# Attention sums accumulated key tile by key tile, or all at the end of a batch

## The chip, the cores and the metric

The kernel runs on one core of a Trainium2 chip. A core has five engines that take their instructions in order, each from a queue of its own, and that wait for each other through semaphores: TensorE (PE in the profile; its weight loads are PEld), VectorE (DVE), ScalarE (ACT), GpSimd (POOL) and SyncE (SP), which here issues nearly all transfers. The metric is device time in microseconds (us), the median of several runs; less is better.

## The reference

The input is x of shape (32, 512, 128) and a symmetric 0/1 adjacency of shape (32, 512, 512). Four layers follow each other, each as x = x + layer(relu(layernorm(x)), adjacency). The change lies in the first, an attention whose mask is the adjacency:

```
v = relu(x Wv + bv);  q = relu(x Wq + bq);  k = relu(x Wk + bk)
h = clip((q k^T) * mask, 0, CLAMP_HI) - NEG_PENALTY * (1 - mask)
out = softmax(h, axis=2) @ v
```

The second layer is a graph convolution with an LSTM over 128 rows, taken from the last 128 nodes of each batch; the third is four graph layers with tanh; the fourth is a product with the adjacency and a PReLU. For the change it matters that the attention of one query is a sum over the 512 keys of exp(score) times mask times v, divided by the sum of exp(score) times mask.

## The kernel before, in words

The path that runs is `symmetric` (line 772); `general` (line 39) is a fallback for other inputs. The work of the 32 batches is cut in four:

- `pass_1(b)` (line 1126) computes keys and values of a batch and the attention of its last 128 queries alone, which the LSTM needs, and stores keys, values and normed input in DRAM (f_dkq, f_dv).
- `lstm()` (line 1220) makes 128 steps for all batches together. A step is a chain from engine to engine: a product on PE (f_z, line 1234), tanh on ACT (1260, 1272), two cell operations on DVE (1266, 1267), tanh on ACT (1274), and the output with its transpose on DVE (1278, 1279), after which the next step's product can start.
- `pass_2(b)` (line 1289) does the attention of the other 384 queries, in three tiles of 128. It loads the stored data and the mask, makes the queries (f_pq, 1316, and f_q, 1319 or 1320), and for each of the four key tiles j a scores product (f_s, 1325), its exponential on ACT (f_e, 1328), and the mask on DVE (1329). Then come twelve products with the values (f_po, 1334): for each query tile t, four that add up over j. The values carry a column of ones, so that the sum of the exponentials comes out in column 128. DVE takes its reciprocal (1338) and updates x (1340), which is stored as f_dx (1345). For batches 0 to 21 (`EARLY`), the sums over the graph (f_pg, 1419) are made in pass 2 too.
- `rest(b, turn, ...)` (line 1433) does all that needs the LSTM's result. The first two turns take batches 26 and 27 (`FIRST`). Its steps that matter here are f_plw and f_pl (1470, 1477), f_gT (1481), a norm, the turned rows f_xt_c (872), and per graph layer f_py (1523, its bank filled with a bias by line 967 or 971), f_y (1402, 1403), f_pa (1419, 1530, 1534). It also stores the adjacency (f_das, 1491), reads it back transposed (f_aT, 1493), and compares both on DVE (f_junk, 1496).

Each f_s, f_pq, f_po and f_z product is split by `quarters` (or `products`) into four products over 32 columns of PE, which fill one quarter of the output's partitions each and run side by side. [...]one f_po product shows as eight matmul records in the profile.

The order on each queue is written out by a planner, `Plan` (line 522). Every operation has a rank, an assumed time on each engine that may run it, and the tiles that it reads and writes. `Plan.run` (607) places the operations one after the other, each time the one that can start first by these assumed times. LSTM steps have ranks under 1000 and go first; pass 2 has 20000 and up; the last four batches (`LATE`) and the rest have 30000 and up. Operations with the same rank go by their number, that is, by the order in which the code creates them. An operation that is the first to use a tile needs a free buffer of its tag. Tags that matter here are "mm", eight PSUM banks; "n0" to "n2" (four each) and "y" (five), which hold exponentials; "ar" (six), which holds squared adjacencies and also the masks of batches 28 to 31; and "x" (seven). `room` (675) keeps banks back for the LSTM and for what is next in rank. DMA issues on SP in the stretch of pass 2 are tied to the LSTM's steps by `hold_back` (599).

Of the kernel before, what the change touches and what calls it, by code (L numbers as in the profile page):

```python
# [13 lines left out]
P = 128  # L14
# [757 lines left out]
def symmetric(ctx, tc, x, adj, weights, cols, rows, lstm_b, prelu_a, out, fail):  # L772
# [12 lines left out]
    nc = tc.nc  # L785
    B, N, D = x.shape
    NT = N // P
    T = P
    L = NT - 1
# [30 lines left out]
    def flat(ap):  # L820
        return ap.rearrange("p a b -> p (a b)")

    def f32(ap):
        return ap.bitcast(FP)
# [5 lines left out]
    def new(tag, shape, name, dtype=FP):  # L830
        return plan.cell(sb, tag, shape, dtype, name)

    def bank(name, shape=(P, 512), whole=True, filled=False):
        return plan.cell(ps, "mm", shape, FP, name, whole, filled)


    def t_mm(n):
        return max(0.222, n * 0.001676)
# [6 lines left out]
    def t_act(n):  # L845
        return 0.17 + n * 0.0006

    def t_dve(n):
        return 0.145 + n * 0.00088
# [4 lines left out]
    def PE(rank, t, fn, r=(), w=(), **k):  # L854
        return plan.op({"PE": (t, fn)}, rank, r, w, **k)

    def ACT(rank, t, fn, r=(), w=(), **k):
        return plan.op({"ACT": (t, fn)}, rank, r, w, **k)

    def DVE(rank, t, fn, r=(), w=(), **k):  # L860
        return plan.op({"DVE": (t, fn)}, rank, r, w, **k)

    def POOL(rank, t, fn, r=(), w=(), **k):
        return plan.op({"POOL": (t, fn)}, rank, r, w, **k)

    def DMA(rank, kb, fn, r=(), w=(), **k):
        return plan.op({"SP": (max(0.45, t_dma(kb)), fn)}, rank, r, w, gap=k.pop("gap", 2.0), **k)
# [175 lines left out]
    def ln_stats(rank, xc, tiles, name, at=0):  # L1043

        st = new("st", (P, NT, 6), f"f_st_{name}")
        mv = new("mv", (P, NT, 2), f"f_mv_{name}")
        for t in tiles:
            DVE(rank, 0.19, lambda t=t: nc.vector.bn_stats(st.t[:, t, :], xc.t[:, t - at, :]), [(xc, t - at)], [(st, t)])
        for t in tiles:
            DVE(rank, 0.09, lambda t=t: nc.vector.bn_aggr(mv.t[:, t, :], st.t[:, t, :]), [(st, t)], [(mv, t)])  # L1050
        return mv

    def ln_rstd(rank, mv, a, b, rs):

        def fn():
            nc.gpsimd.tensor_scalar_add(rs[0](), mv.t[:, a:b, 1], EPS_LN)
            nc.gpsimd.tensor_tensor(rs[0](), rs[0](), neg_half[:, 0, a:b], OP.pow)
        POOL(rank, 0.78 + 0.13 * (b - a), fn, [mv], [rs[1]])
# [226 lines left out]
    def quarters(product):  # L1285
        for k in range(P // TURN):
            product(slice(k * TURN, (k + 1) * TURN))

    def pass_2(b):
        R = 20_000 + b * 10 if b < B - LATE else 30_000 + (b - B + LATE) * 10 + 15  # L1290
        dkq, dv, dl, dx = kept[b]
        early = b in EARLY
        whole = early or b in FIRST
        a = new("a" if whole else "ar", (P, NT, N if whole else NR), f"f_a_{b}")
        keys = new("inv", (P, N), f"f_k2_{b}")
        hT = new("xn", (P, NR), f"f_h2_{b}")
        v = new("n3", (P, NT, P + 1), f"f_v2_{b}")
        xc = new("x", (P, NT if whole else L, P), f"f_x2_{b}")
        DMA(R, 192, lambda: nc.sync.dma_start(hT.t, dkq.t[:, N:]), [dkq], [hT], gap=LANDED)
        DMA(R, 256, lambda: nc.sync.dma_start(keys.t, dkq.t[:, :N]), [dkq], [keys], gap=LANDED)  # L1300
        if whole:
            for t in range(NT):
                DMA(R, 256, lambda t=t: nc.sync.dma_start(a.t[:, t, :], adj[b, t * P : (t + 1) * P, :]), [], [(a, t)], gap=LANDED)
            ar, deg = squares(R, b, a, "2")
            mask, rows_of = ar, lambda j: f32(ar.t[:, j, :NR])
        else:
            for t in range(NT):
                DMA(R, 192, lambda t=t: nc.sync.dma_start(a.t[:, t, :], adj[b, t * P : (t + 1) * P, :NR]), [], [(a, t)], gap=LANDED)
            mask, rows_of = a, lambda j: a.t[:, j, :]
        DMA(R, 258, lambda: nc.sync.dma_start(v.t, dv.t), [dv], [v], gap=LANDED)  # L1310
        DMA(R, 192, lambda: nc.sync.dma_start(xc.t[:, :L, :], x[b, :NR].rearrange("(t p) d -> p t d", p=P)), [],
            [(xc, t) for t in range(L)], gap=LANDED)
        if whole:
            DMA(R, 64, lambda: nc.sync.dma_start(xc.t[:, L, :], dl.t), [dl], [(xc, L)], gap=LANDED)
        pq = bank(f"f_pq_{b}", (P, NR), whole=False)
        PE(R, t_mm(NR), lambda: quarters(lambda p: nc.tensor.matmul(pq.t[p], w[:, W_Q, p], hT.t, start=True, stop=True)), [hT], [pq], tiled=True)  # L1316
        q = new("xn", (P, NR), f"f_q_{b}")
        plan.op({
            "ACT": (t_act(NR) + 0.09, lambda: nc.scalar.activation(q.t, pq.t, AF.Relu, bias=colb[:, C_Q : C_Q + 1])),
            "DVE": (t_dve(NR), lambda: nc.vector.tensor_scalar(q.t, pq.t, colb[:, C_Q : C_Q + 1], 0.0, OP.add, OP.max)),  # L1320
        }, R, [pq], [q])
        es = []
        for j in range(NT):
            s = bank(f"f_s_{b}_{j}", (P, NR), whole=False)
            PE(R, t_mm(NR), lambda s=s, j=j: quarters(lambda p: nc.tensor.matmul(  # L1325
                s.t[p], keys.t[:, j * P + p.start : j * P + p.stop], q.t, start=True, stop=True)), [keys, q], [s], tiled=True)
            e = new(f"n{j}" if j < 3 else "y", (P, NR), f"f_e_{b}_{j}")
            ACT(R, t_act(NR), lambda s=s, e=e: nc.scalar.activation(e.t, s.t, AF.Exp), [s], [e])  # L1328
            DVE(R, t_dve(NR), lambda e=e, j=j: nc.vector.tensor_mul(e.t, e.t, rows_of(j)), [(mask, j)], [e])
            es.append(e)  # L1330
        po = bank(f"f_po_{b}", (P, L, P + 1), whole=False)
        for t in range(L):
            for j in range(NT):
                PE(R, t_mm(P), lambda t=t, j=j: quarters(lambda p: nc.tensor.matmul(  # L1334
                    po.t[p, t, :], es[j].t[:, t * P + p.start : t * P + p.stop], v.t[:, j, :], start=(j == 0), stop=(j == NT - 1))),
                    [es[j], v], [po], tiled=True)
        ri = plan.fixed(None)
        sum_ops.append(DVE(R, 0.21, lambda: nc.vector.reciprocal(rinv[:, b, :L], po.t[:, :, P]), [po], [ri]))
        for t in range(L):
            DVE(R, 0.26, lambda t=t: nc.vector.scalar_tensor_tensor(xc.t[:, t, :], po.t[:, t, :P], rinv[:, b, t : t + 1],  # L1340
                                                                    xc.t[:, t, :], OP.mult, OP.add), [po, ri], [(xc, t)])
        if whole and not early:
            begun[b] = a, xc, ar, deg
        else:
            DMA(R + 5, 192, lambda: nc.sync.dma_start(dx.t, xc.t[:, :L, :]), [(xc, t) for t in range(L)], [dx], gap=STORED)
        mv = ln_stats(R, xc, range(L), f"r{b}")
        l1 = lns[b]
        POOL(R, 0.15, lambda: nc.gpsimd.tensor_copy(ln1[:, b, 0, :L], mv.t[:, :L, 0]), [mv], [(l1, "mr")])
        ln_rstd(R, mv, 0, L, (lambda: ln1[:, b, 1, :L], (l1, "rr")))
        if early:  # L1350
            d = new("dg", (P, NT), f"f_d2_{b}")

            def root():
                nc.gpsimd.tensor_scalar_add(d.t, deg.t, 1.0)
                nc.gpsimd.tensor_tensor(d.t, d.t, neg_half[:, 0, :], OP.pow)
            POOL(R, 1.3, root, [deg], [d])
            rs = new("rs", (P, NT), f"f_rs_2{b}")
            POOL(R, 0.34, lambda: nc.gpsimd.tensor_mul(rs.t, ln1[:, b, 1, :], d.t), [d, l1], [rs])
            gT, _ = sums_of_1(R, b, xc, ar, rs)
            dg = plan.fixed(dram.tile([P, N], FP, tag=f"g{b}", name=f"f_dgT_{b}"))  # L1360
            DMA(R + 5, 256, lambda: nc.sync.dma_start(dg.t, flat(gT.t)), [gT], [dg])
            kept_sums[b] = dg
# [5 lines left out]
    def squares(rank, b, a, name):  # L1368

        ar = new("ar", (P, NT, N), f"f_ar{name}_{b}", FR)  # L1370
        deg = new("dg", (P, NT), f"f_deg{name}_{b}")
        for t in range(NT):
            ACT(rank, 0.62, lambda t=t: nc.scalar.activation(ar.t[:, t, :], a.t[:, t, :], AF.Square,  # L1373
                                                             accum_out=deg.t[:, t : t + 1]), [(a, t)], [(ar, t), (deg, t)])
        return ar, deg
# [338 lines left out]
```

## Time and profile before

| | us |
|---|---|
| median of 3 runs (lowest to highest) | 1305.71 (1305.48 to 1306.47) |
| time of the profiled execution | 1305.92 |
| its span, first to last instruction | 1304.0 |
| first LSTM product (f_z) starts | 181.8 |
| last LSTM step ends | 505.2 |
| f_po records, first to last start | 172.8 to 514.4 |

The span is 1.9 us shorter than the time of the same execution; what lies around it is the same for both kernels. Up to 182 us the profile shows pass 1, from there to 505 us the LSTM with pass 2 in between its steps, and from there on the rest. A row of a group of instructions gives their count, the mean time of one, and how long the engine was idle just before them and for whom. Records of PE overlap, since its products are pipelined: four quarters of 273 ns each take about as long as one. What a product costs is therefore read from the chain of waits, where consecutive records are merged.

### The profile page before, as it was taken

The numbers are of one execution on the slowest core, as the hardware profiler recorded it, in microseconds if no ns is written. First come the engines' busy times: TensorE is split into PE (matmuls) and PEld (weight loads), VectorE is DVE, ScalarE is ACT, GpSimd is POOL, SyncE is SP. The second block draws the span as 40 slices with busy tenths as digits, with TensorE's granted clock in tenths as the row PEclk, the third lists the DMA queues.
The fourth block names the chain that finished last, engine by engine and source line by source line (L and its number), as shares of the span: only waits on it lengthen the run. The fifth ranks groups of instructions, "written<-read, shape, count | busy, mean of one in ns | idle before, by whom it ended". The sixth has DMA issues, their size and how long they took to land.

```text
span 1304.0 us, 32965 instructions
## 1 busy us (share of the span) xinstructions
PE 1268.1 (97%) x12087; PEld 976.6 (75%) x12087; DVE 990.3 (76%) x3284; ACT 830.2 (64%) x2079; POOL 389.8 (30%) x733
## 2 busy tenths in 40 slices
PE   9999999998999999899999999999999999999997
PEld 6888876666766677677778787787777877877774
DVE  7989878877978787587667677676776787787754
ACT  5666667777777554577566676666766665675423
POOL 4654533222222133232213223132231322332000
PEclk9999999999999999899999999999999999999998
DMA  8888888887746655889476667666676366673311
GB/s 259 270 275 285 265 271 273 257 262 252 246 140 215 209 182 139 198 191 243 103 152 156 155 163 163 154 159 154 162 160 144 86 136 145 139 170 65 50 33 35
DMA packets 300699, 232.03 MB, mean 178 GB/s; under 512 B 140656, under 2 KB 246128, under 8 KB 300528
## 3 DMA queue, kind: packets, MB, share of 16 engines
q1 hardware_dynamic: 283632, 213.06, 58.4%
q0 software_dynamic: 16896, 16.78, 8.4%
q8 instruction: 97, 1.59, 0.5%
q14 instruction: 74, 0.61, 0.2%
HBM read 136.19 MB, written 62.13 MB: 152 GB/s over the span
## 4 chain that ended last, share of the span: by engine, by line
PE 85%; DVE 5%; DMA 3%; ACT 2%; issue 2%; POOL 1%; SPq 0%; ACTq 0%; DVEq 0%
PE f_pa L1419 17%; PE f_py L1523 14%; PE f_pa L1534 14%; PE f_pg L1419 8%; PE f_po L1334 5%; PE f_s L1325 5%; PE f_z L1234 4%; PE f_pk L1141 2%; PE f_pol L1184 2%; PE f_pv L1157 2%; PE f_p L1575 2%; PE f_sl L1174 2%; PE f_pl L1477 2%; PE f_pd L1209 2%; PE f_pq L1316 1%
## 5 line engine op out<-in xcount | busy, mean ns | idle before, releaser
L1419 PE MATMUL f_pa<-f_ar,f_y 128*128 128x512 f32 x1024 | 295.6, 426 | 0.7 <-ACT f_y L1402 0.7
L1419 PEld LDWEIGHTS f_pa<-f_ar,f_y 128*128 128x128 f32 x1024 | 189.4, 188 | 72.1 <-issue 37.3
L1523 PE MATMUL f_py<-f_wf,f_n 128*128 128x128 f32 x1280 | 175.0, 276 | 0.0
L1523 PEld LDWEIGHTS f_py<-f_wf,f_n 128*128 128x128 f32 x1280 | 165.4, 192 | 9.3 <-ACT f_n L1538 1.4
L1534 PE MATMUL f_pa<-f_n,f_wf 128*128 128x512 f32 x320 | 153.0, 593 | 0.3 <-DVE f_pa L1530 0.3
L1538 ACT ACTIVATE f_n<-f_pa,f_bcol 128x512 f32<-128x512 f32 x128 | 88.3, 690 | 93.5 <-PE f_pa L1534 93.4
L1373 ACT ACTIVATE f_ar<-f_a 128x512 fp32r<-128x512 f32 x216 | 133.6, 621 | 5.3 <-PE f_pg L1419 3.1
L1402 ACT CAST f_y<-f_py 128x512 fp32r<-128x512 f32 x128 | 74.7, 584 | 93.7 <-PE f_py L1523 88.4
L1491 POOL DMA_DIRECT2D f_das<-f_ar x32 | 27.8, 868 | 354.0 <-ACT f_ar L1373 284.5
L1334 PE MATMUL f_po<-f_v,f_e 128*32 128x129 f32 x3072 | 106.3, 274 | 6.0 <-issue 5.9
L1334 PEld LDWEIGHTS f_po<-f_v,f_e 128*32 128x32 f32 x3072 | 89.3, 110 | 20.4 <-issue 13.2
L1403 DVE TENSOR_TENSOR f_y<-f_py,f_y 128x512 fp32r<-128x512 f32 x128 | 87.4, 686 | 22.0 <-ACT f_y L1402 21.8
L1325 PE MATMUL f_s<-f_q,f_k 128*32 128x384 f32 x1024 | 100.6, 490 | 0.0
L1530 DVE TENSOR_TENSOR f_pa<-f_pa,f_inv 128x512 f32<-128x512 f32 x128 | 86.6, 693 | 16.5 <-PE f_pa L1419 16.1
L1234 PE MATMUL f_z<-f_w,f_seq 128*32 128x128 f32 x2040 | 85.1, 277 | 10.6 <-DVE f_seq L1279 4.2
L1534 PEld LDWEIGHTS f_pa<-f_n,f_wf 128*128 128x128 f32 x320 | 57.9, 190 | 47.1 <-issue 37.7
L1234 PEld LDWEIGHTS f_z<-f_w,f_seq 128*32 128x32 f32 x2040 | 55.4, 109 | 48.1 <-issue 11.4
L1496 DVE SCALAR_TENSOR_TENSOR f_junk<-f_a,f_aT 128x1024 bf16<-128x1024 f32 x64 | 78.1, 1221 | 7.1 <-DMA f_aT<-f_das 6.1
L1419 PE MATMUL f_pg<-f_ar,f_xp_d 128*128 128x512 f32 x256 | 75.3, 417 | 0.3 <-DVE f_xp_d L1411 0.2
L1523 PE MATMUL f_py<-f_wf,f_T_c 128*128 128x128 f32 x448 | 72.9, 275 | 0.0
L1328 ACT ACTIVATE f_e<-f_s 128x384 f32<-128x384 f32 x128 | 60.8, 484 | 17.7 <-PE f_s L1325 9.9
L1096 DVE COPY f_hl_d<-f_n 128x1024 uint16<-128x1024 uint16 x28 | 19.4, 694 | 68.8 <-ACT f_n L1538 68.8
(197 smaller groups left out, 2756.8 us busy)
## 6 DMA issues: line engine op xcount, KB each, us to landing
f_a<-in_adj_dram SPq DMA_DIRECT2D x30, 1024.0 KB
f_a<-in_adj_dram SPq DMA_DIRECT2D x96, 256.0 KB
f_das<-f_ar POOLq DMA_DIRECT2D x32, 512.0 KB, 4.8
f_dkq<-f_kh SPq DMA_DIRECT2D x32, 448.0 KB
f_dv<-f_v SPq DMA_DIRECT2D x32, 258.0 KB
f_v<-f_dv SPq DMA_DIRECT2D x32, 258.0 KB
f_x<-in_x_dram SPq DMA_DIRECT2D x32, 256.0 KB
f_al<-in_adj_dram SPq DMA_DIRECT2D x32, 256.0 KB
```

The costliest lines, as they stand in the source:

```text
L1234: nc.tensor.matmul(z.t[part, k, :, :], h, w[:, m : m + 4, part], start=False, stop=True, skip_group_check=True)
L1325: PE(R, t_mm(NR), lambda s=s, j=j: quarters(lambda p: nc.tensor.matmul(s.t[p], keys.t[:, j * P + p.start : j * P + p.stop], q.t, start=Tru ...
L1334: PE(R, t_mm(P), lambda t=t, j=j: quarters(lambda p: nc.tensor.matmul(po.t[p, t, :], es[j].t[:, t * P + p.start : t * P + p.stop], v.t[:, ...
L1373: ACT(rank, 0.62, lambda t=t: nc.scalar.activation(ar.t[:, t, :], a.t[:, t, :], AF.Square, accum_out=deg.t[:, t : t + 1]), [(a, t)], [(ar, ...
L1402: ACT(rank, t_act(N), lambda: nc.scalar.copy(parts.t[:, :, 0, :], src.t), [src], [(parts, 0)])
L1403: DVE(rank, t_dve(N), lambda: nc.vector.tensor_sub(parts.t[:, :, 1, :], src.t, f32(parts.t[:, :, 0, :])), [src, (parts, 0)], [(parts, 1)])
L1419: nc.tensor.matmul(pg.t, parts.t[:, j, k, :], ar.t[:, j, :], start=(k == 0 and j == 0), stop=(k == 1 and j == NT - 1))
L1496: nc.vector.scalar_tensor_tensor(junk, flat(a.t[:, 2 * k : 2 * k + 2, :]), 1.0, flat(aT.t[:, 2 * k : 2 * k + 2, :]), OP.mult, OP.not_equal ...
L1523: nc.tensor.matmul(py.t[:, j, :], nodes[n].t[:, bass.ts(j, P)], wf[:, W_F[i] + c, 0, :], start=False, stop=(c == nch - 1), skip_group_chec ...
L1530: before = DVE(R, t_dve(N), lambda pa=pa: nc.vector.tensor_mul(pa.t, pa.t, inv_row.t), [inv_row], [pa])
L1534: nc.tensor.matmul(pa.t, wf[:, W_F[i] + c, 1, :], nodes[n].t, start=False, stop=(c == nch - 1), skip_group_check=True)
L1538: ACT(R, 0.57, lambda pa=pa, n=n, i=i: nc.scalar.activation(n.t, pa.t, AF.Tanh, bias=bcol[:, i : i + 1]), [pa], [n])
```

## The change

The bank for the sums is taken before the loop over key tiles. Inside the loop, right after the mask, three products (one per query tile) add key tile j's part. So the order of the twelve is by key tile and then query tile, where it was by query tile and then key tile. The three query tiles' sums are now open at once in one bank, so that only the very first product of a quarter carries the start flag. The list of exponential tiles is gone. Nothing else is edited; since operations are numbered in the order of the code and the planner places them by what is ready, the order on all queues can move.

```diff
-        es = []
+        po = bank(f"f_po_{b}", (P, L, P + 1), whole=False)
         for j in range(NT):
...
             e = new(f"n{j}" if j < 3 else "y", (P, NR), f"f_e_{b}_{j}")
             ACT(R, t_act(NR), lambda s=s, e=e: nc.scalar.activation(e.t, s.t, AF.Exp), [s], [e])
             DVE(R, t_dve(NR), lambda e=e, j=j: nc.vector.tensor_mul(e.t, e.t, rows_of(j)), [(mask, j)], [e])
-            es.append(e)
-        po = bank(f"f_po_{b}", (P, L, P + 1), whole=False)
-        for t in range(L):
-            for j in range(NT):
-                PE(R, t_mm(P), lambda t=t, j=j: quarters(lambda p: nc.tensor.matmul(
-                    po.t[p, t, :], es[j].t[:, t * P + p.start : t * P + p.stop], v.t[:, j, :], start=(j == 0), stop=(j == NT - 1))),
-                    [es[j], v], [po], tiled=True)
+            for t in range(L):
+                PE(R, t_mm(P), lambda e=e, t=t, j=j: quarters(lambda p: nc.tensor.matmul(
+                    po.t[p, t, :], e.t[:, t * P + p.start : t * P + p.stop], v.t[:, j, :], start=(j == 0 and t == 0),
+                    stop=(j == NT - 1), skip_group_check=True)), [e, v], [po], tiled=True)
```

## The prediction

> **What bounds the kernel now.** I read the totals first, then a table by stage, then the instructions of the sums, the timeline where their stage ends.
>
> ```profile
> PE 1268.1 (97%) x12087; PEld 976.6 (75%) x12087; DVE 990.3 (76%) x3284; ACT 830.2 (64%) x2079; POOL 389.8 (30%) x733
> ```
>
> TensorE (PE) is busy for 97% of a span of 1304.0 us. The stages, with the columns us, then busy us and count of PE, PEld, DVE, ACT, POOL, then granted clock, DMA share, GB/s:
>
> ```profile
> 182.00:342.00 160.00, 152.57 (x3091) 107.98 (x3087) 132.79 (x540) 122.03 (x432) 43.98 (x84) 1.00 0.84 262
> 342.00:504.00 162.00, 152.80 (x3304) 107.54 (x3295) 132.79 (x565) 101.90 (x363) 39.15 (x78) 0.99 0.60 185
> 504.00:700.00 196.00, 190.26 (x1078) 148.35 (x1077) 136.60 (x373) 121.86 (x273) 57.47 (x94) 0.98 0.76 174
> 700.00:900.00 200.00, 200.00 (x1099) 157.53 (x1098) 145.01 (x375) 133.89 (x284) 54.36 (x84) 1.00 0.68 157
> ```
>
> From 504 us on PE is the bound, to the last microsecond. From 182 to 504, the LSTM, it isn't: 16.6 us of 322 are idle.
>
> ```profile
> L1334 PE MATMUL f_po<-f_v,f_e x3072: 270/273/422, 172.8 to 514.4; 128*32 128x129 f32 x192
> L1329 DVE TENSOR_TENSOR f_e<-f_e,f_a x32: 516/550/559, 435.4 to 505.2; 128x384 f32<-128x384 f32 x32
> L1279 DVE STREAM_TRANSPOSE f_seq<-f_h x128: 211/211/216, 185.0 to 504.9; 128x32 f32<-128x32 f32 x128
> ```
>
> The last row ends each LSTM step. Its 128 starts, taken from the timeline of VectorE (DVE), lie 2.08 to 5.33 us apart, median 2.32, sum 319.9. The sums (first row) and the masking of late batches (second) end with the LSTM. So pass 2 is filler in a chain of steps: filler that fits costs nothing, and filler left over lands where PE is full. Right behind the LSTM, though, PE waits:
>
> ```profile
> 512.43 2.20 PE L1334 MATMUL f_po<-f_v,f_e 128*32 128x129 f32 x72
> 518.87 1.13 PE L1523 MATMUL f_py<-f_wf,f_hT_c 128*128 128x128 f32 x8 [0.92 <-DVE f_py L971]
> 520.67 2.14 PE L1419 MATMUL f_pa<-f_ar,f_y 128*128 128x512 f32 x8 [0.67 <-ACT f_y L1402]
> 524.69 1.22 DVE L1496 SCALAR_TENSOR_TENSOR f_junk<-f_a,f_aT 128x1024 bf16<-128x1024 f32 x1 [3.35 <-DMA f_aT<-f_das]
> 526.59 2.08 PE L1534 MATMUL f_pa<-f_hT_c,f_wf 128*128 128x512 f32 x2 [3.78 <-DVE f_sh_c L1076]
> ```
>
> PE idles 0.92 + 0.67 + 3.78 = 5.4 us; the longest wait comes from a DVE queue that stands before a late transfer.
>
> ```profile
> 526.00:529.00 3.00, 2.41 (x5) 1.27 (x6) 3.00 (x7) 1.18 (x3) 0.00 (x0) 0.50 0.43 130
> ```
>
> The granted clock (third from the end) is 0.50 then. Over 522 to 528 it averages 0.78, over 528 to 534 0.65; in 526.6 to 528 half and in the last six 35% is lost: some 2.8 us.
>
> [...]3.78 us idle, then 0.50. [...]the trace has LSTM weight loads waiting 7.1 us, 16 times, for work on the exponentials' tiles. [...]with POOL's store and SP's loads together the DMA share in 510 to 516 is full.
>
> **The change part by part.** *The products.* 32 x 12 before and after, same operands and shapes. A product is 8 records; 48 records took 1.33 us of the chain, so 0.22 us. The sum is 0. The reversed order loads the same weights, since each product has its own. *Latency of a batch.* Behind the last exponentials stood 9 products, now 3: 6 x 0.22 = 1.3 us sooner. I price it at nothing: the reciprocal waited for sums only 6.3 us in all, 7 times, off the end's path. *Buffers.* The bank was taken at the first product and is still; tiles of exponentials come free sooner.
>
> *The order.* The planner places products by readiness and free banks, so I compared both kernels' written orders on each engine. That of PE agrees up to the second but last scores product of pass 1 (171.5 us). Then:
>
> (a) *LSTM start.* Before the first LSTM product stood 8 scores products and 13 sums, now 4 and 12. DVE had three pieces between the last pass-1 sum and its reciprocal besides one masking: another masking 0.5, f_q 0.61, the diagonal 0.68; they move behind it. The reciprocal, at 175.96, could follow its sum at 174.85, and the convolution, held at 180.06 by three scores products (hp done at 178.97), can start about 177.7. The first LSTM product moves up 2.3 to 2.4 us: **-2.4**. Cover gone, it is 0.
>
> (b) *LSTM length.* I added filler per step from the rows' prices (sum 0.22, scores or f_pq 0.65, f_pg 2.04) and set it beside the measured interval. Filler under 2.0 us: mean 2.43; 2.0 to 2.15: 2.61; 2.15 to 2.4: 2.87; above: 3.40. Steps in the last three classes: 10, 5, 9 before, 13, 4, 6 after. Over the lowest class's mean that is 3 x 0.18 - 1 x 0.44 - 3 x 0.97 = -2.8, say **-3**. But 11 steps were long for reasons other than filler, about 12.5 us in all, such as 2.3 us at 471 in which PE waited for nothing that shows; a new order meets those anew, so -6 to +4.
>
> (c) *Behind the LSTM.* There stood 9 sums, now 48: all four late batches (28 to 31), whose scores are still done in the LSTM. The reason is on SP: their masks take buffers of the tag ar, which come free only as the last f_pg of early batches run, and these move from steps 105 and 106 into 126 and 127. So 39 x 0.22 = **+8.6** us of PE work comes to where PE is full. Along come on DVE 15 maskings x 0.55 = 8.2 us and three batches of updates (0.18 + 3 x 0.30 + 3 x 0.22 + 0.30 = 2.0 each), 14 us; and on SP two batches of masks, three of x and three stores, 14 x 0.19 MB = 2.7 MB, 10 us at the 270 GB/s of busy slices, with as much as 1.5 MB in the last steps before. What waits behind them on SP: the transposes f_aT and the loads of adjacency for the next turns; on DVE: f_sh_c, the bias fill f_py and f_pa of the first turn.
>
> How much of the 8.6 falls into the old idle time? At best 30 of the 39 stand ahead of PE's 526.6. I add up DVE's new queue from 505.2: the fill is done at 521.8 in place of 518.7, f_pa at 529.4, so that product starts at 529.5, +2.9; 9 sums are left, +2.0[...]: **+2.1**. At worst the transfers are as late again, idle time and slow clock recur, and all 8.6 is paid. I take the worst end: the same DVE queue got 14 us longer and the same DMA rings 10 us.
>
> Sum: -2.4 - 3.0 + 8.6 = +3.2 on the profiled execution's 1305.92, which is 0.2 above the median 1305.71: **1309.0** us.
>
> **The rivals.** *Absorbed, no change (0.28).* The upper path: -2.4 - 3.0 + 2.1 = -3.3, and half of (b) lost to new stalls: 1304. For it: transposes now come sooner in SP's order, since the load of x that held them till 519.25 stands behind. Against: the traffic.
> *Absorbed, faster (0.22), the other side.* A place, 505 to 535 us: the 39 sums fill the idle 5.4 us and keep PE awake, and (b) holds in full: 1305.7 - 3.3 - up to 3 of further stall time, about 1300. It decides if f_junk no longer waits for f_aT, that is if the first transpose lands before DVE is through its maskings, about 522.
> *Pile-up (0.12).* The masks come so late that DVE's in-order queue holds the first two turns, PE idles over 6 us more, and the adjacency of the next turns is late too: +10 and above, 1316.
> *The edit does nothing*: not open, since the order of PE changes.
>
> **How the numbers follow.** The forecast has 0.38, the others as above. Within 0.2% (2.6 us) is about what a measurement of this kernel can tell from no change. Forecast and pile-up are slower, 0.50; absorbed splits into same 0.28 and faster 0.22. The range holds forecast, no change and most of faster: 1300 to 1316, both ends of (b) and (c) in it. The forecast's own is 1307 to 1312.
>
> **What would show it.** (a) The first f_z starts near 179.4 and not at 181.8. (b) The ends of steps span 313 to 320 us. (c) The last f_po runs near 530 and not 514; 48 products, 384 of its records, come behind the last f_z, and maskings on DVE reach past 525. If f_junk still waits on f_aT and the clock falls to 0.5 near 530, the forecast holds; if PE shows under 2 us idle between 505 and 540 and clock 1.0, a rival does. I'm wrong if LSTM steps change by more than 6 us, or if later turns, which I take as unchanged, lose time.

## The result, and the profile after

The changed kernel took 1309.84 us (median of six runs, 1306.57 to 1314.09), beside 1304.78 us for the kernel before in six runs: ratio 1.0042, 95% interval 1.0024 to 1.006. Measured again later with nine runs it was 1.0049 (1.0029 to 1.0068). It is slower by 0.4%, and the forecast was 1309.0 us.

The stages after, with the same windows and columns as before (us; busy us and count of PE, PEld, DVE, ACT, POOL; granted clock, DMA share, GB/s):

```profile
504.00:700.00 196.00, 187.28 (x1257) 144.52 (x1248) 141.38 (x389) 115.28 (x261) 60.23 (x97) 1.00 0.78 181
700.00:900.00 200.00, 200.00 (x1098) 157.37 (x1097) 144.56 (x374) 133.73 (x283) 53.96 (x83) 1.00 0.69 157
```

The changed stage is the one from 504 to 700 us: TensorE is busy for 187.28 us where it was for 190.26, so it is idle for 8.7 us where it was for 5.7. From 700 us on the busy times agree within 0.5 us.

The three groups of instructions that showed where pass 2 ends (times in ns, then first and last start in us):

```profile
L1331 PE MATMUL f_po<-f_v,f_e x3072: 270/273/298, 170.7 to 533.6; 128*32 128x129 f32 x192
L1329 DVE TENSOR_TENSOR f_e<-f_e,f_a x32: 517/550/560, 424.1 to 528.2; 128x384 f32<-128x384 f32 x32
L1279 DVE STREAM_TRANSPOSE f_seq<-f_h x128: 211/211/215, 181.3 to 493.9; 128x32 f32<-128x32 f32 x128
```

The LSTM now begins 3.7 us earlier and ends 11 us earlier (493.9, was 504.9), but the sums go on to 533.6 (was 514.4) and the masks of the last batches to 528.2 (was 505.2). What comes with them is seen on SP's queue, first before, then after:

```profile
484.16 1.30 SPq L1308 DMA_DIRECT2D f_a<-in_adj_dram  x3
...
492.53 2.66 SPq L1308 DMA_DIRECT2D f_a<-in_adj_dram  x4
```

```profile
489.75 0.83 SPq L1308 DMA_DIRECT2D f_a<-in_adj_dram  x2
...
493.25 2.69 SPq L1308 DMA_DIRECT2D f_a<-in_adj_dram  x4
...
498.58 3.95 SPq L1308 DMA_DIRECT2D f_a<-in_adj_dram  x4
...
506.31 7.29 SPq L1490 DMA_TRANSPOSE f_aT<-f_das  x2
...
514.75 1.41 SPq L1308 DMA_DIRECT2D f_a<-in_adj_dram  x3
```

Line 1308 with x4 is one late batch's mask. Before, the first two batches' masks were issued by 470 us and the last one at 492.5, twelve us ahead of the LSTM's end. After, all sixteen loads (3.1 MB) are issued between 489.75 and 516 us, where the LSTM has ended at 494. VectorE and TensorE wait accordingly:

```profile
507.27 0.56 DVE L1329 TENSOR_TENSOR f_e<-f_e,f_a 128x384 f32<-128x384 f32 x1 [2.73 <-DMA f_a<-in_adj_dram]
514.16 1.23 DVE L1493 SCALAR_TENSOR_TENSOR f_junk<-f_a,f_aT 128x1024 bf16<-128x1024 f32 x1 [0.57 <-DMA f_aT<-f_das]
```

```profile
509.55 0.64 PE L1331 MATMUL f_po<-f_v,f_e 128*32 128x129 f32 x14 [1.04 <-issue]
520.59 1.12 PE L1531 MATMUL f_pa<-f_hT_c,f_wf 128*128 128x512 f32 x2 [1.49 <-DVE f_pa L1527]
526.56 1.16 PE L1520 MATMUL f_py<-f_wf,f_hT_c 128*128 128x128 f32 x8 [1.50 <-ACT f_py L967]
561.70 0.71 PE L1520 MATMUL f_py<-f_wf,f_n 128*128 128x128 f32 x4 [1.01 <-ACT f_n L1535]
```

The one long wait of before (3.78 us, with the clock at 0.50 from 525.3 to 532.1 us) is gone; the comparison f_junk waits 0.57 us for its transpose and not 3.35. In its place stand many waits of 0.8 to 1.5 us, as far as 622 us.

For all runs I cut the time in four at three marks: the start of the first and of the last L1279, and the third group of f_p products (groups over 3.5 us apart), the one of the third turn. The last stretch, from there to the last f_p group, is 653.9 us before and after; the three before it carry the difference. "Behind" counts from 0.2 us after the last L1279 starts. The next two columns say how long, within that stretch, PE was idle and how long the granted clock was 0.50.

| profile | first step | LSTM | behind | PE idle in it | clock 0.50 in it | time of all runs: ratio (95%) |
|---|---|---|---|---|---|---|
| before | 185.0 | 319.9 | 135.0 | 5.7 | 6.8 | 1 |
| after | 181.3 | 312.6 | 146.6 | 8.6 | 0.0 | 1.0042 (1.0024 to 1.006) |
| after, again | 183.4 | 315.4 | 147.3 | 7.9 | 3.4 | 1.0049 (1.0029 to 1.0068) |
| same plan, new order | 183.7 | 317.5 | 135.0 | 6.5 | 3.4 | 0.9989 (0.9973 to 1.0005) |
| new order at batch's end | 183.6 | 315.1 | 143.7 | 9.0 | 6.8 | 1.0042 (1.0025 to 1.0059) |
| before, sums deferred | 185.8 | 321.0 | 142.6 | 9.3 | 10.2 | 1.0088 (1.006 to 1.0116) |
| after, sums ahead | 182.0 | 323.0 | 135.9 | 6.3 | 3.4 | 1.0012 (0.9997 to 1.0026) |
| before, 36 sums less | 185.4 | 318.5 | 136.3 | 7.7 | 6.8 | 0.9986 (0.9974 to 0.9997) |
| before, comparison later | 184.5 | 321.1 | 134.5 | 4.7 | 3.4 | 0.9987 (0.9973 to 1.0) |
| after, 36 sums less | 182.1 | 317.8 | 146.0 | 14.1 | 6.8 | 1.0052 (1.0039 to 1.0066) |
| after, no masking | 182.2 | 311.3 | 145.2 | 7.3 | 0.0 | 1.0042 (1.0024 to 1.0059) |
| after, no masking, no mask loads | 181.3 | 313.8 | 144.0 | 6.0 | 3.4 | 0.9998 (0.998 to 1.0016) |
| after, neither sums nor masks | 182.5 | 316.9 | 141.6 | 10.4 | 3.4 | 1.0004 (0.999 to 1.0018) |
| after, seven ar buffers | 213.9 | 335.4 | 137.6 | 12.4 | 13.7 | 1.0405 (1.0371 to 1.0438) |

A profile is one execution. Kernels with the same plan up to the LSTM's end differ by as much as 2.1 us in the first column and 6.5 us in the second, while "behind" repeats within 0.7 us (146.6 and 147.3; 135.0 twice). So I use means for the first two, over the profiles that share a plan: before, same plan and comparison later give 184.4 and 319.5; after, again, and the four with something left out give 182.1 and 314.6. (The kernel before with 36 sums less is not among them, since most of its missing sums lay inside the LSTM.) "Behind" holds slow clock too, and not the same amount in each profile: 6.8 us at half the clock can cost up to 3.4 us there by my estimate (two f_pa products of the same shapes took 2.08 us at 0.50, at 526.59 us before, and 1.12 us at 1.00, at 520.59 us after), and before has 6.8 where after has none. So the extra of the changed kernel is, if anything, larger than the 11.6 us between the two.

### The profile page after: what moved, and what is told of

Its sections match the earlier page's. It is cut to its first block, busy times and chain, and to the rows that moved or that the text cites. A ratio compares the mean times of both kernels' runs of the same rounds, so it can differ in the third digit from the quotient of the medians.

```text
span 1304.7 us, 32990 instructions
## 1 busy us (share of the span) xinstructions
PE 1266.0 (97%) x12087; PEld 968.1 (74%) x12088; DVE 995.0 (76%) x3290; ACT 824.1 (63%) x2073; POOL 392.8 (30%) x733
## 4 chain that ended last, share of the span: by engine, by line
PE 79%; DVE 7%; DMA 6%; ACT 4%; POOL 2%; issue 1%; SPq 1%; ACTq 0%; POOLq 0%; DVEq 0%
PE f_pa L1416 16%; PE f_py L1520 14%; PE f_pa L1531 14%; PE f_pg L1416 8%; PE f_s L1325 4%; PE f_z L1234 4%; PE f_po L1331 3%; DMA f_a<-in_adj_dram 3%; PE f_p L1572 2%; PE f_pk L1141 2%; PE f_pl L1474 2%; PE f_pv L1157 2%; PE f_pol L1184 2%; PE f_sl L1174 2%; PE f_pd L1209 1%
## 5 line engine op out<-in xcount | busy, mean ns | idle before, releaser
L1068 ACT ACTIVATE f_xn_c<-f_x,f_sh_c,f_rs_c 128x128 f32<-128x128 f32 x135 | 57.0, 486 | 26.7 <-DVE f_sh_c L1076 26.7
```

## The experiments

**Is it the order of the products, or the plan?** The new order is put into the slots that the planner gave to the old one.

```diff
+                kt, kj = (t * NT + j) % L, (t * NT + j) // L
-                PE(R, t_mm(P), lambda t=t, j=j: quarters(lambda p: nc.tensor.matmul(
+                PE(R, t_mm(P), lambda t=kt, j=kj: quarters(lambda p: nc.tensor.matmul(
```

> Before's plan, slot for slot, with only the twelve products of a batch handed out key tile by key tile in the slots that the planner gave to the old order (still all at the end of the batch). Theory Plan (what changes is where the planner puts the work, not what a product costs): within 1.5 us of before, ratio 0.999 to 1.001, first LSTM step at 181.8 us and last at 505 us as before. Rival Order (accumulating three sums in turn, or switching the operand at every product, costs TensorE time): the 384 products take longer than 0.22 us each, and the kernel is about 5 us slower, ratio 1.003 to 1.005.

Measured 0.9989 (0.9973 to 1.0005), 135.0 us behind as before. Three sums open at once in a bank cost nothing that shows; the plan is the cause.

The new order at the end of the batch, after all four masks, as the planner sees it:

```diff
-        for t in range(L):
-            for j in range(NT):
+        for j in range(NT):
+            for t in range(L):
```

> The products stay at the end of the batch, but are given to the planner in key tile order; it then moves 39 of the last four batches' sums behind the LSTM (before 9, changed kernel 48) and puts 12 sums and 5 scores ahead of it. Theory Plan: the LSTM starts about 2 us earlier and ends 4 to 8 us earlier, the stretch behind it is 6 to 9 us longer, total 1 to 5 us slower than before, ratio 1.001 to 1.004. Rival Inside the loop (only products planned between the scores do harm): same time as before, ratio 0.999 to 1.001.

Measured 1.0042, 143.7 us behind. The place inside the loop over key tiles isn't needed: a swap of two for statements is enough to make the planner put 39 of these sums behind the LSTM, and it costs what the whole change costs.

**Do deferred sums cost, and does it help to have them ahead?** First the kernel before, all 48 late sums made to wait for the last step; then the changed kernel with another constant, which turns the planner's choice.

```diff
-                    [es[j], v], [po], tiled=True)
+                    [es[j], v], [po], after=end if b >= B - LATE else (), tiled=True)
```

> Before's loop and order, with one wait added in the planner: all 48 sums of the last four batches are planned behind the last LSTM step (before: 9). Four aggregations of about 2 us come ahead into the LSTM in their place (40 behind it instead of 44). Theory Deferred sums cost by themselves (late masks and sums behind the LSTM leave TensorE idle there): 3 to 8 us slower, ratio 1.002 to 1.006, and idle of TensorE behind the LSTM up from 5.7 us. Rival Work is only traded (8.6 us of sums go behind, 8.2 us of aggregations come ahead): within 1.5 us of before, ratio 0.999 to 1.001.

```diff
-    LANDED = 3.8
+    LANDED = 3.4
```

> The changed kernel with one constant of the planner altered (a load counts as landed 3.4 instead of 3.8 us after it is issued): the planner then leaves 6 sums of the last four batches behind the LSTM instead of 48, and the filling work within the LSTM is 230.7 us instead of 223.0 by its reckoning. Theory Deferred sums cost: the LSTM is 5 to 9 us longer than in the changed kernel, the stretch behind it 9 to 12 us shorter, total 2 to 6 us faster than the changed kernel, ratio to before 0.997 to 1.001. Rival Work is only traded, and the loss is elsewhere: as slow as the changed kernel, ratio 1.003 to 1.006.

Deferring cost 1.0088, some 11 us and more than the 3 to 8 expected, though four aggregations (f_pg) went ahead in exchange. So the work was traded nearly one for one: the LSTM lost 8.6 us of sums, got 8.2 us of aggregations and kept its length (321.0), while the stretch behind grew by 7.6 us. The loss there is idle time (9.3 us for 5.7) and slow clock (10.2 us at 0.50 for 6.8), which speaks for the theory. TensorE's longest wait was

```profile
529.24 1.24 PE L872 MATMUL f_xt_c<-f_ident,f_xn_c 128*128 128x128 f32 x4 [4.74 <-DVE f_xn_c L1065]
```

Putting them ahead gave 1.0012: behind, 135.9 us, 11 less than in the changed kernel; in the LSTM, 8.4 more than the changed kernel's mean, for 7.7 us of added filler by the planner's reckoning. So, by this one profile, about three quarters of the gain was paid back inside the LSTM. That last part I had expected (5 to 9 us), but it speaks against filler that costs nothing.

**What does a late sum cost by itself?** 36 of the 48 are left out, in either kernel, without a change of plan.

```diff
+                one = b >= B - LATE
-                PE(R, t_mm(P), lambda t=t, j=j: quarters(
+                PE(R, t_mm(P), lambda t=t, j=j, one=one: None if one and j != t else quarters(
```

> The kernel before, plan unchanged, with 36 of the 48 sums of the last four batches left out (only the products of each query tile with its own key tile are made, so those batches' attention is incomplete): 29 of the 36 lay within the LSTM and 7 behind it. Theory Free within the LSTM (a sum of 0.22 us fits into what a step leaves open on TensorE): the LSTM keeps its length within 2 us, the stretch behind it loses 1.5 us, ratio to before 0.9975 to 0.9995. Rival Same price everywhere: the LSTM is 6.4 us shorter as well, about 8 us in all, ratio 0.993 to 0.995.

> The changed kernel, plan unchanged, with the same 36 sums left out (those batches' attention is incomplete); all 36 lie behind the LSTM. Theory Full price behind the LSTM: the stretch behind it is 8 us shorter (36 x 0.22) than in the changed kernel, ratio to before 0.997 to 0.999. Rival The masks and loads that come with the deferred sums are what delays, not the sums: TensorE waits where it worked, the gain is under 3 us, ratio to before 1.002 to 1.004.

Before: 0.9986, 1.8 us (0.4 to 3.4) for 36 sums, the LSTM shorter by 1 us of 6.4; with the plan kept, sums in the LSTM are almost free. (The stretch behind, 136.3, didn't get shorter by the 1.5 us expected. And the 8.4 us of the run with sums ahead, which has another plan, stand against this 1 us; what makes the difference is open.) After: 1.0052, nothing gained at all, and this is the run that overturned my account. The time behind stays at 146.0 us; TensorE waits where it worked, 14.1 us instead of 8.6:

```profile
513.48 1.15 PE L1332 MATMUL f_po<-f_v,f_e 128*32 128x129 f32 x16 [4.63 <-issue]
516.64 0.66 PE L1332 MATMUL f_po<-f_v,f_e 128*32 128x129 f32 x8 [2.01 <-DVE f_e L1329]
```

Right behind the first of these waits the granted clock was 0.50, from 513.5 to 520.4 us, while TensorE was busy for 4.8 us. So up to 2.4 us, an estimate from half of that busy time, of what the missing sums could have given went to the slow clock, and the run shows that taking them out gains nothing, not that they took no time. The chain of work that ended last, in this run, goes through the load of a mask (start us, us, what):

```profile
504.92 7.88 DMA f_a<-in_adj_dram
512.82 0.41 DVE f_e L1329
513.47 0.45 DVE f_e L1329
...
516.64 0.66 PE f_po L1332 x8
...
529.49 5.09 DMA f_x<-f_dx
534.61 2.56 ACT f_ar L1371 x8
```

**Where do the changed kernel's runs differ among themselves?** Together with the two above ran the changed kernel once more, and the kernel before with the transposing loads of the first two turns given 8 us to land, so that the comparison stands later.

> The changed kernel once more, for a second profile and more times. Its first profile was its fastest execution, 3.3 us below its median. Theory The spread is in the LSTM: the stretch from the last step to the third turn stays at 146 to 147 us and the LSTM is 2 to 4 us longer than 312.6 us. Rival The spread is behind the LSTM (loads of masks landing late): the LSTM stays at 312 to 313 us and the stretch behind is 2 to 4 us longer. Ratio to before 1.003 to 1.006 in both.

The spread is not behind the LSTM: 147.3 after 146.6, while the first step came 2.1 us later and the LSTM was 2.8 us longer. The first profile had simply caught the fastest execution. In the second one f_junk waits 1.26 us, and the clock is 0.50 from 528.0 to 531.4 us, which the first doesn't show.

```diff
-        plan.op({"SP": ...}, R + 2, [das], [aT], gap=4.0)
+        plan.op({"SP": ...}, R + 2, [das], [aT], gap=8.0 if turn < 2 else 4.0)
```

> The kernel before, with the transposing loads of the first two turns counted by the planner as landing 8 us after their issue instead of 4, so that the comparisons which wait for them stand later on VectorE; everything up to the end of the LSTM is planned as before. Theory The idle behind the LSTM is what absorbs or exposes work there: the 3.8 us wait of TensorE at 522.8 us and the slow clock after it (2.8 us) go, 3 to 6 us faster, ratio 0.995 to 0.998. Rival The next thing is late there too: within 1.5 us of before.

0.9987 (0.9973 to 1.0): 1.7 us and not 3 to 6. The wait of 3.78 us is gone, and 0.5 us of the stretch with it. The slow clock isn't gone, though, only halved (3.4 us at 0.50 for 6.8), and smaller waits came up later (0.97 and 0.74 us at 574 and 586 us). So the idle time on which my rivals and my two ends of step (c) turned was worth little, as far as this run removed it.

**Masks: the waiting or the loads?** The changed kernel without the sixteen multiplications, then without the loads too. (Both have, besides the lines shown, a guard that lets the code which ties SP's issues to the LSTM's steps skip a load that isn't made.)

```diff
-            DVE(R, t_dve(NR), lambda e=e, j=j: nc.vector.tensor_mul(e.t, e.t, rows_of(j)), [(mask, j)], [e])
+            DVE(R, t_dve(NR), lambda e=e, j=j: None if b >= B - LATE else nc.vector.tensor_mul(...), [(mask, j)], [e])
```

> The changed kernel, plan unchanged, with the sixteen mask multiplications of the last four batches left out (their exponentials go unmasked into the sums); the sixteen loads of those masks are still made. Theory Loads (the 3.1 MB of late masks stand ahead of other transfers on SP's queue and on the DMA engines behind the LSTM): hardly a gain, the stretch from the last LSTM step to the third turn stays at 144 to 147 us, ratio to before 1.003 to 1.006. Rival Mask waits (VectorE is held by the masks that have not landed, 3.4 us, and the sums behind it): 3 to 6 us faster than the changed kernel, ratio to before 1.000 to 1.002.

```diff
-                DMA(R, 192, lambda t=t: nc.sync.dma_start(a.t[:, t, :], ...), [], [(a, t)], gap=LANDED)
+                DMA(R, 192, lambda t=t: a.t[:, t, 0] if b >= B - LATE else nc.sync.dma_start(...), [], [(a, t)], gap=LANDED)
```

> As the run without the mask multiplications, and the sixteen loads of the late masks (192 KB each) are left out too. Theory Loads: the other transfers behind the LSTM come earlier, the stretch from the last step to the third turn falls by 6 to 10 us against the run that keeps the loads, ratio to before 0.996 to 1.000. Rival Mask waits: no further gain over the run that keeps the loads, within 2 us of it.

Without the multiplications 1.0042: neither their 9 us of VectorE nor their waits matter. Without the loads 0.9998, and the two intervals don't meet: by the times the loads cost 0.44%, 5.7 us, with an uncertainty of some 2 us. In 494 to 506 us, with the loads and without:

```profile
494.00:506.00 12.00, 12.00 (x221) 10.87 (x223) 6.37 (x24) 6.12 (x16) 3.07 (x4) 1.00 1.08 249
```

```profile
494.00:506.00 12.00, 12.00 (x168) 10.57 (x170) 5.62 (x22) 5.83 (x18) 3.07 (x4) 1.00 0.81 163
```

The transfers that the turns wait for share this time; whether SP's queue or the DMA engines hold them was not separated. But the stretch behind fell only to 144.0 us, by 1 to 3 us and not by 6 to 10 (it has 3.4 us at half the clock, an estimated 1.7 us at most, which the run with the loads hasn't). What the times gained beyond that lies in the first two columns, which vary by as much from one execution to the next; I can't place it.

**Two limits, one under the other?** Both left out at once.

> The changed kernel, plan unchanged, without 36 of the deferred sums and without the sixteen mask multiplications and mask loads of the last four batches: both left out that were left out singly before (those batches' attention is incomplete and unmasked). From the last LSTM step to the third turn the changed kernel took 146.6, without the sums 146.0, without the loads 144.0, the kernel before 135.0 us. Theory Two limits, one under the other (TensorE's own extra work of 9 us, and the loads that take as long beside it; each alone hides the other's removal): the stretch falls to 135 to 138 us and the ratio to before is 0.992 to 0.997. Rival A third limit (other transfers or engines behind the LSTM in this order of work): the stretch stays at 142 us or more and the ratio at 0.998 to 1.003.

Partly. The sums alone were worth 0.9 us of the stretch (146.9, mean of two, to 146.0), the loads alone 2.9, both 5.3: each does hide some of the other. It shows best at the first f_pa of the first turn. From the start of the last L1279 to it pass 26.7 us in the changed kernel, 26.8 without the sums, 25.7 without the loads, but 21.7 without both, and 21.6 before. So up to there these two limits lie one under the other, and no third one shows. In this run:

```profile
L1279 DVE STREAM_TRANSPOSE f_seq<-f_h x128: 211/211/214, 182.5 to 499.4; 128x32 f32<-128x32 f32 x128
521.04 1.12 PE L1532 MATMUL f_pa<-f_hT_c,f_wf 128*128 128x512 f32 x2 [1.59 <-DVE f_pa L1528]
```

But the whole stretch, 141.6 us, is still 6.6 above before, nearly all of it after that f_pa, and the time, 1.0004, is no better than without the loads alone. That is what the rival said: a third limit was there. (With the new order at the batch's end the first f_pa comes after 22.0 us, and yet the stretch is 8.7 us longer than before.) Its place shows on ScalarE, before and in this run:

```profile
560.31 0.63 ACT L1373 ACTIVATE f_ar<-f_a 128x512 fp32r<-128x512 f32 x1 [0.27 <-DMA f_a<-in_adj_dram]
...
561.07 0.69 ACT L1538 ACTIVATE f_n<-f_pa,f_bcol 128x512 f32<-128x512 f32 x1
...
563.71 0.62 ACT L1373 ACTIVATE f_ar<-f_a 128x512 fp32r<-128x512 f32 x1
```

```profile
557.75 0.63 ACT L1371 ACTIVATE f_ar<-f_a 128x512 fp32r<-128x512 f32 x1 [2.82 <-DMA f_a<-in_adj_dram]
...
560.22 0.67 ACT L1536 ACTIVATE f_n<-f_pa,f_bcol 128x512 f32<-128x512 f32 x1
```

```profile
532.31 2.05 PE L1521 MATMUL f_py<-f_wf,f_n 128*128 128x128 f32 x16 [1.22 <-ACT f_n L1536]
560.94 0.71 PE L1521 MATMUL f_py<-f_wf,f_n 128*128 128x128 f32 x4 [1.71 <-ACT f_n L1536]
593.73 3.68 PE L1417 MATMUL f_pa<-f_ar,f_y 128*128 128x512 f32 x8 [2.39 <-ACT f_y L1400]
```

Before, one square of a later turn's adjacency went ahead of the tanh f_n and the others behind it. In the new plan all four stand ahead and wait for a 1 MB load that has not landed, and TensorE waits for the tanh, the third time for the copy f_y behind such squares: three waits, 5.3 us. In the changed kernel itself the waits for ACT after 560 us are 1.0, 0.4, 1.3 and 0.8 us, 3.5 in all, where before had a single one of 0.3, for DVE. This part I read from traces and have not taken away.

**A seventh buffer for masks.**

```diff
-    BUFS = {"a": 2, "ar": 6, "x": 7, "xn": 5, "y": 5, "gs": 5, "inv": 4, "n0": 4, "n1": 4, ...
+    BUFS = {"a": 2, "ar": 7, "x": 6, "xn": 4, "y": 5, "gs": 4, "inv": 4, "n0": 4, "n1": 3, ...
```

> The changed kernel with seven buffers instead of six for squared adjacencies and late masks, paid for with one buffer less of four small kinds. The planner then puts all 48 sums of the last four batches and 3.5 more aggregations into the LSTM or ahead of it (24 sums and 11 scores ahead of the LSTM, no sum behind it). Theory Loads: with the late masks loaded within the LSTM the stretch behind it is 135 us or less; the LSTM starts 2 to 4 us later and is 5 to 9 us longer than in the changed kernel; total 4 to 9 us faster than the changed kernel, ratio to before 0.996 to 1.001. Rival The place of the loads does not matter and each move is paid back: ratio to before 1.003 to 1.006.

A miss: 1.0405. No sum was left behind the LSTM and the stretch was 137.6 us, but the first step came at 213.9 us, 29 later than before, and the LSTM took 335.4: the buffers given up (x, xn, gs, n1) were needed, as I read it; no run gave them back one by one. So it says nothing on the place of the loads, and whether it is the ar buffers that defer the masks was not separately shown.

## Why the prediction was right

The time was: 1309.0 forecast, 1309.84 measured, slower, inside the range. Its steps were not all, and that the sum came so near is in part luck.

- *Step (a), the LSTM's start.* Forecast -2.4. The first f_z starts at 178.8 us (forecast 179.4, before 181.8). By the means over profiles with one plan it starts 1.5 us earlier (179.7 for 181.2), and the first step ends 2.3 us earlier. Right, if somewhat over-sized, and by the named cause: the reciprocal now starts at 173.96 us and the diagonal behind it, at 177.55, and the convolution starts at 177.31 where 177.7 was said.
- *Step (b), the LSTM's length.* Forecast -3, with -6 to +4. Measured -7.3 in the first profile, which is beyond the bounds and beyond the 6 us that I had named as a sign of being wrong, and -4.9 by the means (314.6 against 319.5): right sign, within the bounds, under-sized. The filler of each step was too coarse a ground: two profiles of the changed kernel differ by 2.8 us. No run tests whether filler is what made the steps shorter.
- *Step (c), behind the LSTM.* Forecast +8.6; measured 146.9 - 135.0 = +11.9. The facts of the step hold (48 sums behind, masks to 528, last sum at 533.6 where 530 was said, loads crowding SP, with a DMA share in 504 to 510 and 510 to 516 us of 1.24 and 1.08 where it was 0.45 and 1.15), and its worst end was the right one to take. The best end, +2.1, is 2.9 + 2.0 less 2.8 us of slow clock that I took as won back once the long wait went; that was my estimate, and in the run with the later comparison, without that wait, 3.4 us at 0.50 remained of 6.8. Its price was put on the wrong thing. I charged 39 sums at 0.22 us on a full TensorE. On the books this even fits, since f_po takes 12.2 us of the stretch where it took 2.2. But 36 sums taken away return nothing, because the mask loads hold the first turn as long as the sums do (26.8 us to its first f_pa without the sums, 25.7 without the loads). These loads, which I had listed as a mere reason to choose the worst end, cost 5.7 us by the times, of which the stretch itself shows 1 to 3; without both, the first 21.7 us of it go as before. The new order of the turns' own work, which I had not looked at, is the likely cause of the rest: it leaves waits after 560 us that were 0.3 us before and are 3.5 now. The reading under the step, that PE is the bound from 504 us "to the last microsecond", was wrong at this place.
- *The old idle time.* I said that 5.4 us of idle and 2.8 us of slow clock would recur. The amount did: between 505 and 540 us PE idles 5.2 us, but in waits of 1.5 us and less, and f_junk waits only 0.57 us. The clock stays at 1.00 in the first profile and falls to 0.50 at 528 us in the second, so the two signs that I had named came up in the second execution, f_junk waiting 1.26 us, and not in the first. It also decided less than I thought: without that wait the kernel before gains 1.7 us (0 to 3.5).
- *The sum.* -2.4 - 3.0 + 8.6 = +3.2 against -2.3 - 4.9 + 11.9 = +4.7 by the profiles and +5.1 by the medians. Steps (b) and (c) were both too small and with opposite signs, by 1.9 and 3.3 us; that they cancelled in part is the luck.
- *Later turns unchanged.* Right from the third turn on: 653.9 us before and after.

## What to carry to other kernels

In the stage from 504 to 700 us TensorE was busy 96% (187.28 of 196 us), and the stage was still held by its loads (5.7 us by the times) and, as I read the traces, by the order on another engine (3.5 us of waits for ScalarE after 560 us): added busy time says what an engine did, and only a run without that work says what it cost. Where two limits lie one under the other, a run that takes away one of them shows nothing; take away both. If an edit lets a planner or scheduler move work across a phase border, price the transfers and waits that move with it, and look at the new order of all that follows, before the arithmetic. Where every order of a greedy plan gives another one (a swap of two loops deferred 39 sums, a constant of 3.4 for 3.8 brought them back), a gain or loss of 0.4% belongs to the plan that was drawn, not to the edit.

## What was not expected of the hardware

The granted clock fell on shorter idle than the 3.78 us of before. In the kernel before the clock was already down at 525.3 us, 2.5 us into that wait. In the run with the later comparison waits of 0.93 and 0.68 us that ended at 519.49 and 521.30 us came before a fall, and in the run with neither sums nor masks a single wait of 2.39 us. Here are those two, cut where the clock changes:

```profile
518.48:521.88 3.40, 1.80 (x12) 1.47 (x12) 3.18 (x13) 1.18 (x2) 1.40 (x3) 1.00 0.25 74
521.90:525.30 3.40, 3.40 (x11) 2.48 (x9) 1.68 (x6) 1.50 (x3) 0.67 (x1) 0.50 1.21 233
```

```profile
590.46:593.85 3.39, 1.00 (x4) 0.17 (x3) 0.96 (x2) 3.23 (x9) 0.88 (x3) 1.00 0.85 145
593.87:597.27 3.40, 3.40 (x9) 2.63 (x10) 1.78 (x4) 2.86 (x8) 0.72 (x1) 0.50 0.28 79
```

The changed kernel, with 1.49, 0.19, 0.16 and 1.50 us of idle between 519 and 527 us, stayed at 1.00. So the length of one wait did not tell. What the traces show besides is an even spacing: between the start of a kernel and its end, the clock in each of the 14 profiles changed only at whole multiples of 3.41 us from each other. It was down for 3.41, 6.83 or 10.24 us, and in the kernel before up for 47.79 (14 times 3.41) in between. I cut each profile into such stretches, without the first and last 12 us. Of 5225 stretches at full clock, 20 had PE idle for 2 us or more, and each was followed by half the clock. Of the others four were (just under 2, 1.95, 1.60 and 1.30 us idle); all the rest, with up to 1.95 us, were not. In the kernel before it was two stretches of 371, with 2.27 and 2.51 us of idle, from 470.7 and 521.9 us on; in the changed kernel none of 374, with 1.63 us at most, and its four waits fell into three stretches, with 0.91, 0.99 and 1.50 us of idle. Counted back from the fall at its end (1298.26 us), a border of stretches lies at 526.8 us in the changed kernel's first profile, where the second has one at 528.0 us. That the same waits can therefore halve the clock in one execution and not in the other is my reading; no run separates it.
